# Layer 0 scores of two-block tiles as two half-width products of 64 queries and 192 keys

## The chip, the cores and the metric

The kernel runs on one core of one Trainium2 chip. The metric is the device time in microseconds of one execution. The engines are named as the profile names them: PE is TensorE (PEld its weight loads, which overlap its products), DVE is VectorE, ACT is ScalarE, POOL is GpSimd, SP is SyncE, whose queue issues most DMAs. Each engine runs its own instructions in order and waits for the others by semaphores.

## What is computed

Two transformer layers, both modulated by a conditioning vector, on `x` of 2 batches x 512 positions x 512 channels in float32. Each layer is an attention and a feed-forward part, each behind a layer norm with gain and shift, each added back through a gate. The change touches only the attention of layer 0: 32 query heads share 8 key/value heads, 128 channels a head, with a sliding window of 128 positions.

```python
q = _rope((x @ wq).reshape(B, S, 32, 128), pos)
k = _rope((x @ wk).reshape(B, S, 8, 128), pos)
v = (x @ wv).reshape(B, S, 8, 128)
qg = q.reshape(B, S, 8, 4, 128)
scores = jnp.einsum('bqhgd,bshd->bhgqs', qg, k) * sm_scale
allowed = (j <= i) & (j > i - 128)
scores = jnp.where(allowed[None, None, None], scores, neg)
attn = jax.nn.softmax(scores, axis=-1)
out = jnp.einsum('bhgqs,bshd->bqhgd', attn, v)
return out.reshape(B, S, 32 * 128) @ wo
```

A query at position i sees the keys i-127 to i. For a block of 128 queries these lie in its own block of 128 keys and the one before.

## The kernel before

**Layer 0's attention** (`attention0`, L529) works in 16 units, one for each pair of key/value head and batch. A unit has four blocks of 128 queries (`qb` 0 to 3). The loop over steps `n` (inside `tc.manual_schedule`, L678) takes one block a step and spreads the work of a block over three steps. The order in which it issues is the order of each engine's queue. In step `n` come: `scores` of block `n`; keys, values or queries of the next unit (`keys`, `values`, `queries`, through `roped`, L548); `normalised` of block `n`; `turned` of block `n-1` (transposes of the probabilities); `output` of block `n-2` (projection by `wo`, added to `x`); `mix` of block `n-1` (probabilities times values). At the end of early steps comes one piece of the modulation vectors, popped from `aside`: every third piece is a group of products for the modulation rows (`mod_rows`, L96), the piece after it transposes them (`mod_columns`, L114), and other pieces load weights or spread the gates. In the last units, pieces of layer 0's feed-forward part follow.

So on PE a score tile stands between `mix` of the block before (L650, four 512-column records) and the queries, keys or values of the next unit (L552, L574). Only where an `aside` piece ended the step before does that piece stand ahead of it.

**A score tile** (`scores`, L598). For block 0 there is one key block (`nk` = 128), for the others two (`nk` = 256). For each of the four heads of the unit there is one product: 128 queries as weights, `nk` keys as the moving operand, into the PSUM tile `sp` of 128 x 4 x 256 float32. DVE adds the mask table `band` (L610; 0 where a query may look, -1e30 elsewhere) and takes the negative maximum (L616). ACT takes the exponential with the sum of each row, head by head (L620), into an SBUF tile. `sp` comes from a pool with a single buffer (L543), so the products of a tile can start only when ACT has read the tile before.

In a two-block tile the 128 x 256 scores of a head hold two corners that the mask removes whole: the first 64 queries never see the last 64 keys, the last 64 queries never the first 64 keys.

**Products on part of the columns.** A product whose weights have at most 64 or 32 columns can be put on part of the array's columns, chosen by the PSUM partitions that it writes. The kernel does so in `mod_rows` (L103: 32 weight columns, two products side by side) and in layer 1's `mix` (L1102: 32 columns, four side by side). The profile writes such shapes as 128*32, the full one as 128*128.

**Before the loop** the modulation rows of the first norm, the norm itself and its transposes run, `tables` (L506) loads the rotation table and `band`, and `load_group` (L514) the weights of the first head.

Of the kernel before, what the change touches and what calls it, by code (L numbers as in the profile page):

```python
# [10 lines left out]
F32 = mybir.dt.float32  # L11
F32R = mybir.dt.float32r
I32 = mybir.dt.int32
AF = mybir.ActivationFunctionType
ALU = mybir.AluOpType
AX = mybir.AxisListType
PSUM = bass.MemoryType.PSUM

P = 128
# [4 lines left out]
EPS = 1e-5  # L24

NKV, GRP, HD, WIN = 8, 4, 128, 128

NH, HD1, LAT, ROPE = 128, 4, 64, 64
SCALE1 = float(1.0 / np.sqrt(np.float32(HD1 + ROPE)))
# [13 lines left out]
def adaln_kernel(ctx: ExitStack, tc: tile.TileContext, A: dict, out: bass.AP):  # L43
# [247 lines left out]
    with ExitStack() as c01:  # L291
# [7 lines left out]
        with ExitStack() as c00:  # L299
# [34 lines left out]
            def finale(ap, pool):  # L334
# [31 lines left out]

            norm1 = Norm(1, 0, 1, mid)
            attention0(
                tc, small, hT, xs, gate[2], ident, tabs, groups, load_group,
                lambda pool: [  # L370
# [124 lines left out]
def weights0(tc, A, ctx):  # L495

    nc = tc.nc
    wq = A["L0_attn_wq"].rearrange("(kc p) n -> p kc n", p=P)
    wk = A["L0_attn_wk"].rearrange("(kc p) n -> p kc n", p=P)
    wv = A["L0_attn_wv"].rearrange("(kc p) n -> p kc n", p=P)  # L500
    wo = A["L0_attn_wo"].rearrange("(h p) n -> p h n", p=P)
    QW = GRP * HD
    wp = ctx.enter_context(tc.tile_pool(name="w0", bufs=2))
    tab = ctx.enter_context(tc.tile_pool(name="tab0", bufs=1))

    def tables():  # L506

        rope = tab.tile([P, 4, S], F32, tag="rope", name="rope")
        nc.sync.dma_start(out=rope, in_=A["c_rope"])
        band = tab.tile([P, 2 * P], F32, tag="band", name="band")  # L510
        nc.sync.dma_start(out=band, in_=A["c_band"])
        return rope, band

    def load_group(g):  # L514
        w = {}
        w["k"] = wp.tile([P, KC, HD], F32, tag="wk", name=f"wk{g}")
        nc.sync.dma_start(out=w["k"], in_=wk[:, :, g * HD : (g + 1) * HD])
        w["v"] = wp.tile([P, KC, HD], F32, tag="wv", name=f"wv{g}")
        nc.sync.dma_start(out=w["v"], in_=wv[:, :, g * HD : (g + 1) * HD])
        w["q"] = wp.tile([P, KC, QW], F32, tag="wq", name=f"wq{g}")  # L520
        nc.sync.dma_start(out=w["q"], in_=wq[:, :, g * QW : (g + 1) * QW])
        w["o"] = wp.tile([P, GRP, D], F32, tag="wo", name=f"wo{g}")
        nc.sync.dma_start(out=w["o"], in_=wo[:, g * GRP : (g + 1) * GRP, :])
        return w

    return tables, load_group


def attention0(tc, small, hT, xs, ga, ident, tabs, groups, load_group, aside, finale):  # L529
# [7 lines left out]
    nc = tc.nc  # L537
    rope, band = tabs
    units = [(g, b) for g in range(NKV) for b in range(B)]
    NU = len(units)  # L540
    with ExitStack() as ctx:
        ap = ctx.enter_context(tc.tile_pool(name="a0", bufs=2, reuse_waits="tile"))
        pss = ctx.enter_context(tc.tile_pool(name="pss0", bufs=1, space=PSUM, reuse_waits="tile"))  # L543
        pst = ctx.enter_context(tc.tile_pool(name="pst0", bufs=2, space=PSUM, reuse_waits="tile"))
        pmm = ctx.enter_context(tc.tile_pool(name="psm0", bufs=4, space=PSUM, reuse_waits="tile"))
        kTs, vs, qTs, oTs, sps, pes, pTs = ({} for _ in range(7))

        def roped(dst, wcols, b, tables, name):  # L548

# [44 lines left out]
        def window(qb):  # L594
            k0 = max(qb - 1, 0)
            return k0, (qb + 1 - k0) * P

        def scores(u, qb):  # L598

            k0, nk = window(qb)  # L600
            sp = pss.tile([P, GRP, 2 * P], F32, tag="s", name=f"s{u}_{qb}")
            for hh in range(GRP):
                nc.tensor.matmul(  # L603
                    sp[:, hh, :nk],
                    lhsT=qTs[u][:, hh, qb * P : (qb + 1) * P],
                    rhs=kTs[u][:, k0 * P : k0 * P + nk],
                    start=True,
                    stop=True,
                )
            nc.vector.tensor_add(  # L610
                sp[:, :, :nk],
                sp[:, :, :nk],
                band[:, 2 * P - nk :].unsqueeze(1).to_broadcast([P, GRP, nk]),
            )
            nm = small.tile([P, GRP], F32, tag="nm", name=f"nm{u}_{qb}")
            nc.vector.tensor_reduce(nm, sp[:, :, :nk], AX.X, ALU.max, negate=True)  # L616
            pe = ap.tile([P, GRP, 2 * P], F32, tag="p", name=f"p{u}_{qb}", bufs=3)
            rs = small.tile([P, GRP], F32, tag="rs", name=f"rs{u}_{qb}")
            for hh in range(GRP):
                nc.scalar.activation(  # L620
                    pe[:, hh, :nk], sp[:, hh, :nk], AF.Exp,
                    bias=nm[:, hh : hh + 1], accum_out=rs[:, hh : hh + 1],
                )
            pes[u, qb] = pe, rs
# [53 lines left out]
        with tc.manual_schedule(engines=FOUR):  # L678
            for n in range(-TB, NU * TB + 2):
                u, qb = divmod(n, TB)  # L680
                new = u + 1
                if new < NU and qb == 0 and units[new][1] == 0 and new:
                    groups.append(load_group(units[new][0]))
                if 0 <= u < NU:
                    scores(u, qb)
                if new < NU:
                    if qb == 0:
                        keys(new)
                        queries(new, 0)
                    elif qb == 1:  # L690
                        values(new)
                        queries(new, 1)
                    else:
                        queries(new, qb)
                if 0 <= u < NU:
                    normalised(u, qb)
                before, last = divmod(n - 1, TB), divmod(n - 2, TB)
                if 0 <= n - 1 < NU * TB:
                    turned(*before)
                if 0 <= n - 2:  # L700
                    output(*last)
                if 0 <= n - 1 < NU * TB:
                    mix(*before)
                if aside and n >= -3:
                    aside.pop(0)()
                for f in steps.get(n, ()):
                    f()
# [540 lines left out]
def _constants():  # L1248

    half = HD // 2  # L1250
    inv = np.float32(10000.0) ** (-np.arange(half, dtype=np.float32) / np.float32(half))
    ang = np.arange(S, dtype=np.float32)[None, :] * inv.astype(np.float32)[:, None]
    cos, sin = np.cos(ang).astype(np.float32), np.sin(ang).astype(np.float32)
    co = np.concatenate([cos, cos])

    si = np.concatenate([sin, -sin])
    sm = np.float32(HD**-0.5)
    rope = np.stack([co * sm, si * sm, co, si], axis=1).astype(np.float32)

    i, j = np.arange(P)[:, None], np.arange(2 * P)[None, :]  # L1260
    band = np.where((j > i) & (j <= i + WIN), 0.0, -1e30).astype(np.float32)

    r = np.arange(P) % 16
    lowq = (r // 4 % 2 == 1).astype(np.float32)
    lowk = (r // 8 == 1).astype(np.float32)
    cols = np.zeros((P, 12), np.float32)
    cols[:, 8:] = np.arange(P)[:, None] // 16 % 4 == np.arange(4)[None, :]
    cols[:, 0] = r % 8 < 4
    cols[:, 1] = r % 8 >= 4
    cols[:, 2], cols[:, 3] = 2 * lowq - 1, lowq  # L1270
    cols[:, 4], cols[:, 5] = 2 * lowk - 1, lowk

    i, j = np.arange(P)[:, None], np.arange(P)[None, :]
    blocks = np.arange(P)[:, None] % 16 == np.arange(16)[None, :]
    heads = np.arange(P)[:, None] // 16 % 2 == np.arange(2)[None, :]
    spread = np.stack(
        [(i // 8 == j // 8) & (i % 8 // 2 == 2 * (1 - ty)) for ty in range(2)], axis=1
    ).astype(np.float32)
    n, m = np.arange(N1)[:, None], np.arange(N1)[None, :]
    before = np.broadcast_to((m < n).astype(np.float32), (P, N1, N1)).copy()  # L1280
    expert = np.broadcast_to((np.arange(E1 * R) // R).astype(np.float32), (N1, E1 * R)).copy()
    return {
        "c_rope": rope, "c_band": band, "c_cols": cols, "c_spread": spread,
        "c_block": blocks.astype(np.float32), "c_head": heads.astype(np.float32),
        "c_before": before, "c_expert": expert,
    }
# [46 lines left out]
```

## Time and profile before

| | us |
|---|---|
| median of 3 runs | 2598.6 (2596.83 to 2599.06) |
| the profiled execution, its own time | 2598.26 |
| span of the profiled execution, first to last instruction | 2596.5 |
| PE busy, 60 to 940 us (layer 0's attention and its feed-forward part) | 866.2 of 880 |
| DVE busy there | 460.8 |
| ACT busy there | 178.3 |
| POOL busy there | 306.1 |
| one step of a full unit with two key blocks, 491.19 to 502.38 us (score tile to score tile) | 11.19 |

How to read the profile: the busy time of an engine is the union of its instructions' times. A PE record's duration includes its way through the array, so records of a stream overlap; what a record costs the stream is the distance from its start to the next one's. In the order of time, equal neighbours are merged into one line: start, length from the first start to the last end, engine, line of the kernel, operation, output<-inputs, shape (rows*columns of the array, then the moving operand) and count. A bracket at the end of a line gives the engine's idle time before it and what ended that. In the groups the last figures are busy us, mean ns of one | idle us before. In a list of waits they are us in total, times, longest us.

### The profile page before, as it was taken

The page shows a single profiled execution, that of the slowest core. Times are in us where ns is not written, and L with a number is a line of the kernel's source. Part 1 is how long each engine was busy: PE and PEld are TensorE (multiplying, and loading weights), DVE is VectorE, ACT ScalarE, POOL GpSimd, SP SyncE. Part 2 cuts the span into 40 slices and gives each one's busy share as a digit, 9 for nine tenths or more (in the row PEclk, how much of TensorE's full clock was granted, in tenths as well). Part 3 has the DMA queues.
Part 4 walks back from the last instruction along what each step waited for, and adds up shares of the span by engine and source line. Part 5 has one row for each costly group of instructions (what it writes and reads, how often), then busy time and mean ns, then how long its engine had stood idle before and what let it go on. Part 6 is the DMA issues. An engine that isn't in the chain of part 4 may idle for free.

```text
span 2596.5 us, 32803 instructions
## 1 busy us (share of the span) xinstructions
PE 2501.8 (96%) x12316; PEld 1353.1 (52%) x12316; DVE 1712.8 (66%) x2390; ACT 1443.2 (56%) x2151; POOL 1593.2 (61%) x1538
## 2 busy tenths in 40 slices
PE   7999999999998999999999999999999999999757
PEld 3555555555555445555555555555555555555333
DVE  4455555555555247777778878787877887887642
ACT  2212211211112127888888888888888888888610
POOL 1333334333333315888888888888888888888841
PEclk9999999999999999999999999999999999999868
DMA  6211101101000110000000010000010000000010
GB/s 231 87 57 49 41 9 33 41 7 34 17 1 5 29 32 27 18 25 25 25 25 20 23 29 25 25 17 25 25 29 25 18 24 25 25 29 9 1 31 33
DMA packets 68575, 81.72 MB, mean 31 GB/s; under 512 B 6881, under 2 KB 49536, under 8 KB 68288
## 3 DMA queue, kind: packets, MB, share of 16 engines
q1 hardware_dynamic: 68064, 79.34, 9.8%
q8 instruction: 97, 1.59, 0.3%
q14 instruction: 62, 0.51, 0.1%
q0 software_dynamic: 352, 0.28, 0.0%
HBM read 77.51 MB, written 2.10 MB: 31 GB/s over the span
## 4 chain that ended last, share of the span: by engine, by line
PE 92%; DVE 2%; issue 2%; POOL 1%; ACT 1%; DMA 1%; SPq 0%; POOLq 0%; DVEq 0%; ACTq 0%
PE s L946 20%; PE psq L872 17%; PE acc L1102 9%; PE ps_q L552 8%; PE pw L664 8%; PE s L955 5%; PE s L603 4%; PE po L650 4%; PE psv L574 2%; PE ps_k L552 2%; PE psm L1025 2%; PE pt L639 2%; PE psu L895 2%; PE psf L275 1%; PE psw L1158 1%
## 5 line engine op out<-in xcount | busy, mean ns | idle before, releaser
L1052 POOL TENSOR_TENSOR ss<-ss,row 128x512 f32<-128x512 f32 x512 | 652.8, 1288 | 51.7 <-ACT row L1037 51.3
L965 ACT COPY ss<-s 128x1024 f32<-128x1024 f32 x512 | 506.7, 1013 | 105.6 <-PE s L955 79.9
L1055 ACT ACTIVATE ss<-ss 128x1024 f32<-128x1024 f32 x512 | 530.7, 1066 | 8.0 <-POOL ss L1052 8.0
L872 PE MATMUL psq<-hT,wqr 128*128 128x512 f32 x1024 | 466.9, 599 | 0.1
L620 ACT ACTIVATE p<-s,nm 128x256 f32<-128x256 f32 (+1 forms) x256 | 110.9, 445 | 488.6 <-DVE nm L616 479.8
L972 DVE TENSOR_TENSOR mx<-s,mx 128x1024 f32<-128x1024 f32 x256 | 307.0, 1220 | 97.7 <-PE s L955 96.7
L1046 POOL TENSOR_TENSOR ss<-ss,rowe 128x512 f32<-128x512 f32 x256 | 327.8, 1291 | 2.3 <-ACT rowe L1041 2.3
L562 POOL TENSOR_TENSOR qT<-t_q,t_q 128x512 f32<-128x512 f32 x64 | 81.2, 1269 | 402.6 <-DVE t_q L561 402.6
L872 PEld LDWEIGHTS psq<-hT,wqr 128*128 128x128 f32 x1024 | 189.1, 190 | 242.7 <-issue 216.8
L1102 PE MATMUL acc<-ss,vp 128*32 128x512 f32 x2048 | 266.6, 607 | 7.9 <-ACT ss L1055 7.8
L946 PE MATMUL s<-qh,chkr 64*128 64x512 f32 x1024 | 243.7, 437 | 10.6 <-ACT ss L965 7.4
L972 DVE TENSOR_TENSOR mx<-s,ss 128x1024 f32<-128x1024 f32 x128 | 156.8, 1225 | 113.3 <-PE s L955 90.5
L664 PE MATMUL pw<-wo,oT 128*128 128x512 f32 x512 | 230.3, 592 | 0.0
L552 PE MATMUL ps_q<-hT,wq 128*128 128x512 f32 x512 | 230.1, 592 | 0.0
L955 PE MATMUL s<-qm,c 64*128 64x512 f32 x1024 | 218.4, 391 | 0.0
L946 PE MATMUL s<-ql,clkr 64*128 64x512 f32 x1024 | 218.2, 391 | 0.0
L946 PE MATMUL s<-qh,clkr 64*128 64x512 f32 x1024 | 218.0, 392 | 0.0
L946 PE MATMUL s<-ql,chkr 64*128 64x512 f32 x1024 | 217.8, 392 | 0.0
L946 PEld LDWEIGHTS s<-qh,chkr 64*128 64x128 f32 x1024 | 105.8, 184 | 154.2 <-issue 77.5
L1015 POOL TENSOR_TENSOR st<-mh,own_block 128x512 fp32r<-128x512 f32 x64 | 67.2, 1050 | 180.5 <-DVE mh L1011 180.5
L977 DVE STREAM_TRANSPOSE mx<-mx 128x1024 f32<-128x1024 f32 x128 | 158.7, 1240 | 2.2
L1048 DVE TENSOR_TENSOR ss<-ss,psm 128x512 f32<-128x512 f32 x256 | 158.2, 680 | 0.7 <-PE psm L1025 0.7
(207 smaller groups left out, 3934.8 us busy)
## 6 DMA issues: line engine op xcount, KB each, us to landing
wqr<-in_L_attn_Wq_rope_pairs SPq DMA_DIRECT2D x64, 512.0 KB
wmod<-in_L_wmod SPq DMA_DIRECT2D x12, 1024.0 KB
wq<-in_L_attn_wq SPq DMA_DIRECT2D x8, 1024.0 KB
wo<-in_L_attn_wo SPq DMA_DIRECT2D x8, 1024.0 KB
x<-in_L_attn_x SPq DMA_DIRECT2D x8, 256.0 KB
wk<-in_L_attn_wk SPq DMA_DIRECT2D x8, 256.0 KB
wv<-in_L_attn_wv SPq DMA_DIRECT2D x8, 256.0 KB
wT<-in_L_ffn_WT SPq DMA_DIRECT2D x2, 1024.0 KB
```

Of the source, the lines that this page charges most:

```text
L552: nc.tensor.matmul(ps, lhsT=wcols(kc), rhs=hT[b][:, kc, :], start=(kc == 0), stop=(kc == KC - 1))
L664: nc.tensor.matmul(ps, lhsT=oTs[u][:, hh, i * P : (i + 1) * P], rhs=groups[g]["o"][:, hh, :], start=(hh == 0), stop=(hh == GRP - 1),)
L872: nc.tensor.matmul(ps, lhsT=wqs[t][:, kc, pair * P : (pair + 1) * P], rhs=hT[b][:, kc, :], start=(kc == 0), stop=(kc == KC - 1),)
L946: nc.tensor.matmul(out[:, j, :], lhsT=k[b]["kr"][r, bass.ts(i, P)], rhs=q[t, p][r, :], start=(n == 0), stop=False,)
L955: nc.tensor.matmul(out[:, j, :], lhsT=qkc[t // 2, 1][r, bass.ts(i, P)], rhs=qm[t, p][r, :], start=False, stop=True,)
L965: nc.scalar.copy(ss[t, i, p], hold["s", t, i, p])
L972: nc.vector.tensor_max(mx[t, p], hold["s", t, i, p], before)
L977: nc.vector.transpose(m, m)
L1046: nc.gpsimd.tensor_sub(s, s, hold["r", t, 2])
L1052: nc.gpsimd.tensor_sub(s, s, hold["r", t, 2 * p + 1])
L1055: nc.scalar.activation(ss[t, i, p], ss[t, i, p], AF.Exp)
L1102: nc.tensor.matmul(accs[g, b][32 * h : 32 * (h + 1), :], lhsT=vps[t][:, kb, h, :], rhs=ss[t, kb, h // 2][:, h % 2, :], start=(s == 0 and k ...
```

## The change

In a tile with two key blocks, each head's product of 128 queries with 256 keys becomes two: queries 0 to 63 with keys 0 to 191, and queries 64 to 127 with keys 64 to 255. Each has 64 weight columns and writes 64 PSUM partitions. Tiles with one key block keep their single product of 128 queries and 128 keys, but write it into the right half of `sp`.

The corners that are no longer computed must not reach the maximum and the exponential. So `sp` is made once, ahead of the loop, and filled with -1e30 by DVE; the mask table has 0 in these corners, so that adding it leaves -1e30 there. A one-block tile writes its scores into columns 128 to 255, where one of the two corners lies; its own mask, which is now a third block of `band`, sets that corner back to -1e30. All 128 partitions and all `nk` columns are added, reduced and exponentiated as before. The offsets move: the valid columns start at `o` = 256 - `nk`.

```diff
+H2 = P // 2
+NEVER = -1e30
...
-        band = tab.tile([P, 2 * P], F32, tag="band", name="band")
+        band = tab.tile([P, 3 * P], F32, tag="band", name="band")
...
+        sp = pss.tile([P, GRP, 2 * P], F32, tag="s", name="scores")
+        nc.vector.memset(sp, NEVER)
...
             k0, nk = window(qb)
-            sp = pss.tile([P, GRP, 2 * P], F32, tag="s", name=f"s{u}_{qb}")
-            for hh in range(GRP):
-                nc.tensor.matmul(
-                    sp[:, hh, :nk],
-                    lhsT=qTs[u][:, hh, qb * P : (qb + 1) * P],
-                    rhs=kTs[u][:, k0 * P : k0 * P + nk],
+            o = 2 * P - nk
+            for hh in range(GRP) if qb == 0 else ():
+                nc.tensor.matmul(
+                    sp[:, hh, o:],
+                    lhsT=qTs[u][:, hh, :P],
+                    rhs=kTs[u][:, :P],
                     start=True,
                     stop=True,
                 )
+            for hh in range(GRP) if qb else ():
+                for h in range(2):
+                    lo, hi = h * H2, 2 * P - (1 - h) * H2
+                    nc.tensor.matmul(
+                        sp[h * H2 : (h + 1) * H2, hh, lo:hi],
+                        lhsT=qTs[u][:, hh, qb * P + h * H2 : qb * P + (h + 1) * H2],
+                        rhs=kTs[u][:, k0 * P + lo : k0 * P + hi],
+                        start=True,
+                        stop=True,
+                    )
             nc.vector.tensor_add(
-                sp[:, :, :nk],
-                sp[:, :, :nk],
-                band[:, 2 * P - nk :].unsqueeze(1).to_broadcast([P, GRP, nk]),
+                sp[:, :, o:],
+                sp[:, :, o:],
+                band[:, 0 if qb else 2 * P :][:, :nk].unsqueeze(1).to_broadcast([P, GRP, nk]),
             )
...
-            nc.vector.tensor_reduce(nm, sp[:, :, :nk], AX.X, ALU.max, negate=True)
+            nc.vector.tensor_reduce(nm, sp[:, :, o:], AX.X, ALU.max, negate=True)
...
-                    pe[:, hh, :nk], sp[:, hh, :nk], AF.Exp,
+                    pe[:, hh, :nk], sp[:, hh, o:], AF.Exp,
...
-    band = np.where((j > i) & (j <= i + WIN), 0.0, -1e30).astype(np.float32)
+    band = np.where((j > i) & (j <= i + WIN), 0.0, NEVER).astype(np.float32)
+    band = np.concatenate([band, band[:, P:]], axis=1)
+
+    band[:H2, 2 * P - H2 : 2 * P] = 0.0
+    band[H2:, :H2] = 0.0
```

More of the change, by code (lines that the diff above doesn't have):

```diff
@@ L545, in attention0 @@
         pmm = ctx.enter_context(tc.tile_pool(name="psm0", bufs=4, space=PSUM, reuse_waits="tile"))
-        kTs, vs, qTs, oTs, sps, pes, pTs = ({} for _ in range(7))
+        kTs, vs, qTs, oTs, pes, pTs = ({} for _ in range(6))
+        sp = pss.tile([P, GRP, 2 * P], F32, tag="s", name="scores")
+        nc.vector.memset(sp, NEVER)
         def roped(dst, wcols, b, tables, name):
```

## The prediction

> **What bounds the kernel now.** I read the page's busy shares first, then its chain of waits, then the groups of the stretch in which layer 0's attention runs, its waits, and last the order of time around single tiles. From the page (rows 1 and 4):
>
> ```profile
> PE 2501.8 (96%) x12316; PEld 1353.1 (52%) x12316; DVE 1712.8 (66%) x2390; ACT 1443.2 (56%) x2151; POOL 1593.2 (61%) x1538
> ...
> PE 92%; DVE 2%; issue 2%; POOL 1%; ACT 1%; DMA 1%; SPq 0%; POOLq 0%; DVEq 0%; ACTq 0%
> ```
>
> TensorE is busy for 96% of the span and makes 92% of the chain that ended last; the score products of layer 0 (L603) alone are 4% of that chain. Between 60 and 940 us, groups by form (busy us, mean ns | idle before):
>
> ```profile
> L603 PE MATMUL s<-kT,qT 128*128 128x256 f32 x384 | 91.3, 381 | 0.0
> ...
> L603 PE MATMUL s<-kT,qT 128*128 128x128 f32 x120 | 15.9, 276 | 0.0
> ...
> L103 PE MATMUL psr<-wmod,sc 128*32 128x512 f32 x64 | 14.5, 595 | 0.0
> ```
>
> No idle before any of them. TensorE's own waits in this stretch:
>
> ```profile
> PE po L650 <- ACT pT L641: 8.2, 4, 5.5
> PE pst L193 <- DVE xn L184: 2.8, 1, 2.8
> PE pst L193 <- ACT hT L203: 2.4, 1, 2.4
> ```
>
> That is 13.4 us in 880, the longest (5.5 us at 832 us) in the last unit. So in this stage a microsecond taken from TensorE is a microsecond of the time, except beside those few waits. The clock granted there is 0.99, so the durations need no correction.
>
> One undisturbed step of a two-block tile (the order of time on TensorE; start us, us, line):
>
> ```profile
> 500.66 1.88 PE L650 MATMUL po<-pT,v 128*128 128x512 f32 x4
> 502.38 1.89 PE L603 MATMUL s<-kT,qT 128*128 128x256 f32 x8
> 504.10 3.60 PE L552 MATMUL ps_q<-hT,wq 128*128 128x512 f32 x8
> ```
>
> Durations overlap, so starts count. A float32 product shows as two records. Start to start: four 512-column records in 1.72 us, 0.429 each; eight 256-column records in 1.72 us, 0.216 each. Where 128 columns follow each other (the transposes L639) it is 0.109. So a record costs 2.5 ns + 0.833 ns per column, and one of 192 columns would take 0.1625 us.
>
> The trace has no product on a half of the columns (128*64), but two groups on quarters (128*32): the modulation rows L103, which use two quarters at once, and layer 1's mix L1102, which uses four. One L103 group stands directly between `po` and a score tile:
>
> ```profile
> 199.18 1.88 PE L650 MATMUL po<-pT,v 128*128 128x512 f32 x4
> 200.99 3.63 PE L103 MATMUL psr<-wmod,sc 128*32 128x512 f32 x16
> 204.54 1.99 PE L603 MATMUL s<-kT,qT 128*128 128x256 f32 x8
> 206.37 1.02 PE L552 MATMUL ps_q<-hT,wq 128*128 128x512 f32 x2
> ```
>
> Sixteen 512-column records take 3.55 us, not 16 x 0.429 = 6.86: they run as eight pairs, whose members start 7 ns apart, each pair 0.429 after the last. But both borders cost something. From the single records, to the nanosecond: the last `po` to the first L103 is 0.523 instead of 0.429 (**0.094** more), the first pair to the second 0.453 (0.024 more: the first weights, 32 columns, are not loaded ahead); last pair to first score record 0.528 (0.100 more, of which 7 ns is the stagger), first to second score record 0.320 instead of 0.216 (**0.104** more: 128 columns of weights in the open). The same 0.094 stands at the other changes of array shape that I looked at in layer 1 (0.522 instead of 0.429 from L1102 to L872 and from L872 to L946). The open load is 0.024 for 32 columns and 0.104 for 128, so about 0.051 for 64.
>
> **The change, part by part.**
>
> *The products.* 16 units x 3 tiles = 48 tiles change. Before: 4 heads x 2 records x 0.216 = 1.727 us. After: 4 heads x 2 halves x 2 records of 192 columns; if the halves run as pairs, 8 x 0.1625 = 1.300. That gives back 0.427 us a tile, 20.5 us in all.
>
> *The borders.* Each changed tile now stands alone in another shape: in, 0.094 + 0.051; out, 0.100 + 0.104; together 0.349. Nothing hides this: TensorE is the bound, and the stall is in its own array. 42 tiles therefore gain 0.427 - 0.349 = 0.078 us each, 3.3 us. The other six (steps 2, 3, 5, 6, 9, 11) stand behind an L103 group or behind the 64-row transposes L119 that follow it, and pay for a border already; these take 1.831 us from their first record to the next line now and would take 1.300 + 0.051 + 0.100 + 0.104 = 1.555, a gain of 0.276 each, 1.7 us. Sum 4.9 us; about 0.2 of it falls beside the late 5.5 us wait. I take **4.7 us**.
>
> Here a rule of the Trainium skill speaks against the change. TensorEngine Tiling (Array Packing), Key Properties, says that changing the tiling mode drains the engine, and gives no price. Without it the sum would be -20.5 us; with the row's price it is -4.9. I take the row: the shape differs only in 64 for 32. A second rule, in Instruction Overhead on the same page, puts about 60 cycles on every matmul. At 2.4 GHz (Trainium Kernel Development and Optimization, NeuronCore Architecture), 25 ns, the eight extra records of a tile would cost 0.2 us, 9.6 us over 48 tiles, and turn the sum to +4.9. The trace does not bear it out: the fixed part of a record is 2.5 ns, and a second member of an L103 pair moves the next pair by nothing.
>
> *Weight loads.* 16 loads of 64 columns instead of 8 of 128. By the slope above one takes 0.053 us, so even one after the other a pair's two take 0.107, inside the 0.1625 of the pair before; L103 shows that loads run a pair ahead in this mode. Cost 0; if they were not hidden, up to 0.107 x 7 = 0.7 us a tile.
>
> *The score tile made once.* It was already a single buffer. The waits stay as they were, now perhaps by head: the first product of a tile needs the exponentials of the tile before, which end at 508.7 us for a product at 513.6. Cost 0, cover some 5 us.
>
> *The memset.* One DVE write of 128x1024 to PSUM; the nearest row (L616, the same tile) takes 1.22 us. It can start when the earlier users of these banks are done, near 28.5 us, and would push the first `t_k`; DVE sits idle for 1.34 us before `t_q` at 31.96, and the keys are not used before 57. Cost 0, without that cover 1.2.
>
> *The larger table.* `c_band` grows from 128 to 192 KB: 65.5 KB at the 231 GB/s of the first slice is 0.28 us in front of the weights of group 0. It is still one DMA of SP's queue. The first key product waits for ACT and DVE (`hT`), not for a DMA; cost 0, otherwise 0.3. Add, maximum and exponential keep their sizes; only offsets change.
>
> **Sum.** The profiled execution took 2598.26 us for a span of 2596.5, and lies 0.3 below the median of 2598.6. 2598.26 - 4.7 = 2593.6; against the median 2593.9. **I predict 2593.8 us.** The measurement tells about 0.2% (5.2 us) from no change, so this forecast sits almost on the border, at 2593.4.
>
> **Rivals.**
> - *The borders cost less or nothing* (6%): if the array does not drain between the full shape and halves, up to 20.5 us are gained: 2578. For it: no 128*64 row exists to refute it. Against: every change of shape that I looked at shows the 0.094. With half of them, 48 x 0.175 = 8.4 us more: 2585.
> - *TensorE's instruction supply becomes the bound* (slower, 20%). A changed tile is 32 instructions (16 loads, 16 products) to be started in 1.30 us, 41 ns each. The densest 32 of the trace of before stand in 1.45 us, the densest 64 in 3.29 (45 and 51 ns). If the latter is a rate and not just what that code asks for, a tile's body is 32 x 51 = 1.64 us, 0.34 more: 48 x 0.34 = 16 us more, 2610; at 45 ns 7 us more, 2601. It decides from 0.43 - 0.35 = 0.08 us a tile, a body of 1.38, or 43 ns. Against: at the start of an L1102 group twelve instructions start within 50 ns, so a stock is held, and the `po` before a score tile (8 instructions in 1.7 us) gives time to fill it.
> - *The halves do not run together* (6%): 16 x 0.1625 = 2.60 us a tile, 48 x 1.30 = 62 us more: 2656. For it: no row with 64-column halves. Against: L103 and L1102. A milder form, in which only a product's second record overlaps the next half's first, makes nine rows of eight: +0.16 a tile, 2601.6, still within the border (3%). L103's first pair, started together, speaks against it.
>
> **How the numbers follow.** Forecast 65%, from 2590 to 2597 by the error of the borders (0.05 us a tile is 2.4 us); about half of it lies below 2593.4. Faster by over 0.2%: 0.40 (34 from the forecast, 6 from cheaper borders). Within 0.2%: 0.38 (31 from the forecast, 3 from the milder overlap, 4 from a supply limit near 45 ns). Slower by over 0.2%: 0.22 (16 from the supply limit, 6 from halves one after the other). The range that leaves out no more than 2 in 10 takes the forecast, the mild overlap and most of the supply case: 2588 to 2609; the forecast's own is 2590 to 2597.
>
> **What would show it.** In the profile after: L603 with 128*64 and 192 columns, 768 records; pairs 7 ns apart and 0.1625 us from pair to pair (products right); 0.52 from the last `po` and about 0.21 from the first pair to the second (way in); 0.26 from the last pair to the next line, whose second record is 0.104 late (way out). First record to next line: 1.55 us for 1.73. A pair period of 0.2 or more means supply or loads; single starts mean no overlap. I am wrong if the borders of this shape differ from those of quarters, or if TensorE's waits in the stage grow past 14 us.

## The result and the profile after

| | before | after |
|---|---|---|
| median of 14 runs each, us | 2598.35 | 2592.68 |
| lowest and highest | 2596.83, 2599.49 | 2590.83, 2595.83 |
| span of the profiled execution | 2596.5 | 2591.0 |

The ratio is 0.998, 95% interval 0.9972 to 0.9987: between 3.4 and 7.3 us faster, with the medians 5.7 apart. The forecast was 4.7 us under the profiled execution, and 2593.8 as a time.

The groups by form between 60 and 940 us, after the change (the columns as before; L620 is the product of the halves, L610 that of the one-block tiles, L558 that of the queries, which was L552):

```profile
L620 PE MATMUL scores<-kT,qT 128*64 128x192 f32 x768 | 73.0, 332 | 0.0
L610 PE MATMUL scores<-kT,qT 128*128 128x128 f32 x120 | 15.9, 276 | 0.0
L105 PE MATMUL psr<-wmod,sc 128*32 128x512 f32 x64 | 14.5, 595 | 0.0
L558 PE MATMUL ps_q<-hT,wq 128*128 128x512 f32 x480 | 218.9, 599 | 0.0
```

The queries before:

```profile
L552 PE MATMUL ps_q<-hT,wq 128*128 128x512 f32 x480 | 215.8, 592 | 0.0
```

The 384 records of 256 columns were busy for 91.3 us; the 768 records of 192 columns take 73.0 between them. The difference of 18.3 us is three times what the kernel gained, so the group alone is misleading: part of the cost shows in the lines beside it, as in the 3.1 us more of the queries. One step shows where. The order of time of the profile after, on TensorE, around the same tile as before:

```profile
496.73 1.88 PE L667 MATMUL po<-pT,v 128*128 128x512 f32 x4
498.54 1.52 PE L620 MATMUL scores<-kT,qT 128*64 128x192 f32 x16
499.99 3.70 PE L558 MATMUL ps_q<-hT,wq 128*128 128x512 f32 x8
503.53 1.04 PE L656 MATMUL pt<-ident,p 128*128 128x128 f32 x8
```

Read the starts. From `po` to the scores 1.81 us instead of 1.72: the way in. From the first score to `ps_q` 1.45 instead of 1.72. From `ps_q` to the transposes 3.54 instead of 3.44: the open load on the way out, which now falls into the line behind the tile. Together the stretch is 6.80 us instead of 6.88. TensorE's waits in this stage, after:

```profile
PE po L667 <- ACT pT L658: 8.1, 4, 5.6
PE pst L195 <- DVE xn L186: 2.8, 1, 2.8
PE pst L195 <- ACT hT L205: 1.4, 1, 1.4
```

12.3 us instead of 13.4; nothing new waits.

### The profile page after: what moved, and what is told of

The parts are those of the page before. It is cut to its first block, busy times and chain, and to the rows that moved or that the text cites. A ratio compares the mean times of both kernels' runs of the same rounds, so it can differ in the third digit from the quotient of the medians.

```text
span 2591.0 us, 33543 instructions
## 1 busy us (share of the span) xinstructions
PE 2501.0 (97%) x12700; PEld 1328.9 (51%) x12700; DVE 1712.8 (66%) x2391; ACT 1444.3 (56%) x2151; POOL 1595.1 (62%) x1538
## 4 chain that ended last, share of the span: by engine, by line
PE 92%; DVE 2%; issue 2%; POOL 1%; ACT 1%; DMA 1%; POOLq 0%; DVEq 0%; ACTq 0%
PE s L963 20%; PE psq L889 17%; PE acc L1119 9%; PE ps_q L558 9%; PE pw L681 8%; PE s L972 5%; PE po L667 4%; PE scores L620 3%; PE psv L580 2%; PE ps_k L558 2%; PE psm L1042 2%; PE pt L656 2%; PE psu L912 2%; PE psf L277 1%; PE psw L1175 1%
## 5 line engine op out<-in xcount | busy, mean ns | idle before, releaser
L637 ACT ACTIVATE p<-scores,nm 128x256 f32<-128x256 f32 (+1 forms) x256 | 111.2, 446 | 480.2 <-DVE nm L633 471.2
L558 PE MATMUL ps_q<-hT,wq 128*128 128x512 f32 x512 | 233.3, 598 | 0.0
```

Source lines behind the costliest of these rows:

```text
L558: nc.tensor.matmul(ps, lhsT=wcols(kc), rhs=hT[b][:, kc, :], start=(kc == 0), stop=(kc == KC - 1))
```

## The experiments

Eight runs, all compared with the kernel before on the same chip. Lines and edits refer to the kernel after the change. Per-tile figures are start to start, from the single records of the trace; a float32 product is two records there. The name behind a heading is that by which later texts refer to the run.

**The change without its halves.** (`e1_whole`)

```diff
-            for hh in range(GRP) if qb == 0 else ():
+            for hh in range(GRP):
                 nc.tensor.matmul(
                     sp[:, hh, o:],
-                    lhsT=qTs[u][:, hh, :P],
-                    rhs=kTs[u][:, :P],
+                    lhsT=qTs[u][:, hh, qb * P : (qb + 1) * P],
+                    rhs=kTs[u][:, k0 * P : k0 * P + nk],
...
-            for hh in range(GRP) if qb else ():
-                for h in range(2):
...
-    band[:H2, 2 * P - H2 : 2 * P] = 0.0
-    band[H2:, :H2] = 0.0
```

> The change without its halves: the score tile made once and filled, the wider table and the new offsets stay, but every two-block tile is again one product of 128 queries and 256 keys per head. Theory (the gain is the halves' 0.078 us a tile and nothing else): as before the change, 2598.4 within 1. Rival (the about 1 us by which the measured gain exceeds the sum, 5.7 against 4.7, comes from the other edits, at the start or by finer waits): 2597.4, and the first changed tile again some 0.6 us earlier than before the change.

Measured: 2597.17 us against 2597.55, ratio 1.0 (0.9991 to 1.0008). The single tile, its memset, the wider table and the offsets are worth nothing that these runs can tell; the gain belongs to the halves. The interval of about 2 us on either side can't decide between the theory and the rival's 1 us. The trace helps with the start: here too TensorE reaches the first score tile 0.39 us earlier than in the profile of before, and the first transposes of the modulation (L121) 0.33; in the changed kernel it was 0.27 and 0.70. Up to the first two-block tile the nine traces taken of changed kernels have the same work on TensorE, and they reach it between 65.85 us (the change itself) and 67.23 us (the quarters, second run), for 66.46 before. So such tenths at the start come and go from one execution to the next, and need no edit to explain them.

**The borders alone.** (`e2_wide`)

```diff
-                    lo, hi = h * H2, 2 * P - (1 - h) * H2
+                    lo, hi = 0, 2 * P
...
-    band[:H2, 2 * P - H2 : 2 * P] = 0.0
-    band[H2:, :H2] = 0.0
```

> Halves of 64 queries, but each over all 256 keys: the borders are paid and nothing is saved in the products. Theory (borders 0.349 us a tile for 42 tiles, 0.151 for the six behind an L105 group or its transposes): +15.6 us, 2614. Pairs 0.216 us apart. Rival (borders and open loads depend on the length of the products at their sides): another price than 0.349 in the records, and a time off 2614 by more than 2.

Measured: 2611.94 us against 2597.55, ratio 1.0056 (1.0042 to 1.0069), so 14.4 us slower. Its order of time, `po`, scores and what follows:

```profile
497.71 1.02 PE L667 MATMUL po<-pT,v 128*128 128x512 f32 x2
498.66 1.95 PE L620 MATMUL scores<-kT,qT 128*64 128x256 f32 x16
500.54 2.84 PE L558 MATMUL ps_q<-hT,wq 128*128 128x512 f32 x6
```

Eight pairs, 0.216 us apart, would take 1.727; from the first score to `ps_q` it is 1.878, of which 0.051 is the first open load and 0.100 the border on the way out. With 0.094 ahead of the tile and 0.104 behind, the price of a tile's borders is 0.348 us. It is what rows of 32 columns and of 512 had promised for one of 64 columns beside one of 256: the price doesn't depend on the length of these products. The sum, 15.6 us, is 1.2 above the medians' difference, which is inside the interval (10.9 to 17.9). The 2614 on record is off by 2.1, just past the 2 that the text allowed; it started from 2598.4, and from this group's 2597.55 the sum is 2613.2.

**Quarters.** (`e3_quarters`)

```diff
-H2 = P // 2
+H2 = P // 4
...
-                for h in range(2):
-                    lo, hi = h * H2, 2 * P - (1 - h) * H2
+                for h in range(4):
+                    lo, hi = h * H2, h * H2 + WIN + H2
...
-    band[:H2, 2 * P - H2 : 2 * P] = 0.0
-    band[H2:, :H2] = 0.0
+    for h in range(4):
+        band[h * H2 : (h + 1) * H2, : h * H2] = 0.0
+        band[h * H2 : (h + 1) * H2, h * H2 + WIN + H2 : 2 * P] = 0.0
```

> Four products of 32 queries and 160 keys per head instead of two of 64 and 192. Theory (the stream sets the pace, and four quarters run side by side as in L1119): eight rows of 0.136 us, borders 0.094 + 0.024 + 0.114 + 0.104, 1.42 us a tile instead of 1.727; 15.8 us under before the change, 2582.6. Rival (instruction supply: a tile is 64 instructions in 1.09 us, 17 ns each, while the changed kernel has shown 41 ns each): 64 x 41 ns = 2.6 us for the rows, 1.2 us a tile more than before the change, some 2655; or anything between, with rows wider than 0.136 us after the first stock is used up.

Measured: 2581.69 us against 2597.55, ratio 0.9941 (0.9929 to 0.9954): 15.9 us faster, on the forecast. This settles the supply rival, by a load twice as dense as the change's:

```profile
432.70 1.02 PE L667 MATMUL po<-pT,v 128*128 128x512 f32 x2
433.65 1.29 PE L620 MATMUL scores<-kT,qT 128*32 128x160 f32 x32
434.88 2.41 PE L558 MATMUL ps_q<-hT,wq 128*128 128x512 f32 x5
```

32 product records, and as many weight loads, in 1.22 us. The rows start 0.136 us apart to the last one; nothing widens. The densest 64 instructions of the kernel before (3.29 us) were no rate of the machine, only what that code asked for. That decides it for tiles of this size. Whether a stock of instructions, filled while `po` runs, carries the whole tile is not shown, since no run asks for this density over longer than one tile.

The second run of the same kernel (`e3_again`):

> The quarters once more, beside the two kernels of this group: 2581.7, 15.8 under before the change. Theory and rival as for the first run of it; it serves as the base of e5_turned.

2582.24 us against 2598.26, the same ratio of 0.9941 (0.9928 to 0.9955).

**Another order of the halves.** (`e4_order`)

```diff
-            for hh in range(GRP) if qb else ():
-                for h in range(2):
+            for h in range(2) if qb else ():
+                for hh in range(GRP):
                     lo, hi = h * H2, 2 * P - (1 - h) * H2
```

> The same sixteen half products of a tile in another order: the first halves of all four heads, then the second halves. Theory (products start in the order in which they are issued, and two overlap only where neighbours in that order lie on different column halves): nearly no pairs, sixteen records of 0.1625 us less one overlap, 2.4 to 2.6 us a tile; +1.0 to +1.3 us a tile against before the change, 2648 to 2661. Rival (each half has a queue of its own and takes what is its): pairs as in the change, 2592.7.

Measured: 2625.83 us against 2597.55, ratio 1.0107 (1.0093 to 1.0121). 28 us slower than before, where the theory had 50 or more and the rival a gain: both were wrong.

```profile
504.27 1.02 PE L667 MATMUL po<-pT,v 128*128 128x512 f32 x2
505.22 2.22 PE L620 MATMUL scores<-kT,qT 128*64 128x192 f32 x16
507.37 2.84 PE L558 MATMUL ps_q<-hT,wq 128*128 128x512 f32 x6
```

2.15 us from the first score to `ps_q` for 1.45 in the change; 48 x 0.70 is 33.6 us, and 2592.7 + 33.6 = 2626.3. The starts of this tile's sixteen records fall into two chains with steps of 0.1625 us, each with its own open load at the head:

```
505.223 505.437 505.599 505.762 505.924 506.087 506.249 506.412
505.930 506.143 506.306 506.468 506.631 506.793 506.956 507.118
```

The first chain has to be the first halves, the second the second halves, since a half runs one record at a time. All eight first halves come ahead in the order of issue, yet the second chain starts at 505.930, when the fifth record of the first has just started and three of it have not. So three records can be held back for a busy half while those behind them go to the other; as long as four were held, the other half stood idle. This is also how the change's order gives pairs at all: both records of a head's first half come ahead of those of its second, the second record is held, and the other half starts 7 ns after the first.

**Two heads at a time.** (`e6_twos`)

```diff
-            for hh in range(GRP) if qb else ():
-                for h in range(2):
+            for h2 in range(4) if qb else ():
+                h = h2 % 2
+                for hh in range(2 * (h2 // 2), 2 * (h2 // 2) + 2):
                     lo, hi = h * H2, 2 * P - (1 - h) * H2
```

> The halves in the order first half of heads 0 and 1, second half of heads 0 and 1, then the same for heads 2 and 3, so that four records of one half stand in a row. Theory (from e4_order: the other half starts only when three records of the half in front are still to start, so some three records can be held back): the second half starts together with the first or one record later; 2593 to 2600. Rival (only the next product is held back, and what stands behind it waits): the second half starts two or more records late in each group of four, and a tile takes twelve rows or so: 0.6 us a tile more than the change, some 2622.

Measured: 2594.62 us against 2598.26, ratio 0.9987 (0.998 to 0.9994). Four records of a half stand in a row: one runs, three are held, and the second half starts 13 ns after the first. The tile takes 1.50 us for 1.45. The 0.05 is where the second half turns to heads 2 and 3: there its record is 0.370 us long instead of 0.326 and its next start 0.207 away instead of 0.1625, as behind a load that came late; that cause is not shown. The count of three agrees with both orders; how the hold is built was not tried.

**Transposes right behind the scores,** on the quarters. (`e5_turned`)

```diff
                 if 0 <= u < NU:
                     scores(u, qb)
+                before, last = divmod(n - 1, TB), divmod(n - 2, TB)
+                if 0 <= n - 1 < NU * TB:
+                    turned(*before)
...
-                before, last = divmod(n - 1, TB), divmod(n - 2, TB)
-                if 0 <= n - 1 < NU * TB:
-                    turned(*before)
```

> The quarters, with the transposes of the block before moved up to stand right behind the scores. Theory (the open load on the way out is the first weights of what follows: 0.104 us for 128 columns of a product, 0.055 for a transpose, as in the last unit of the changed kernel, where transposes follow): 0.05 us in each of the 45 tiles that had a product behind them, 2.2 us under the quarters. Rival (the probabilities of the block before, ready by POOL only shortly before, are now waited for, or the copies of the transposes by ACT and DVE come behind the new tile's exponentials and hold up mix): TensorE waits of several us in all, no gain or a loss.

Measured: 2586.18 us, ratio 0.9951 (0.9939 to 0.9964): still faster than before, but slower than the quarters (2582.24 in the same group). Set beside the trace of the quarters' second run, each later step that begins with a two-block tile does gain 0.04 to 0.05 us, as the theory had it; but by step 2 it is 4 us behind. The list of waits from 50 to 100 us has the rival's wait, once:

```profile
PE pt L656 <- POOL p L647: 3.4, 1, 3.4
PE psg L144 <- DVE grow L135: 2.1, 1, 2.1
```

And behind it (stretches with busy time of the engines, then the granted clock, DMA share and GB/s):

```profile
66.00:70.70 4.70, 1.33 (x34) 0.95 (x33) 4.41 (x6) 0.00 (x0) 2.47 (x3) 0.89 0.00 0
70.70:77.50 6.80, 6.80 (x36) 6.80 (x37) 0.18 (x1) 2.41 (x9) 0.00 (x0) 0.57 0.01 2
77.50:84.00 6.50, 6.50 (x22) 2.34 (x22) 2.72 (x5) 0.59 (x1) 0.61 (x1) 1.00 0.14 40
```

Behind the wait the granted clock is 0.57 for 6.8 us. The 32 product records of the values (L580) took 5.9 us there, for 3.7 in the quarters' trace. The rule in the Trainium skill, TensorE: Matmul & The Clock Gate, Part 1, that the clock halves after an idle window of some 3.4 us, fits this wait: behind one of 1.09 us at 819 us in the profile after, the clock is 1.00. The length of a wait alone does not decide, though. Of the two waits of 2.8 us for `xn` in the lists above, the one in the profile before ended at 921.39 us and had 4.9 us at 1.00 behind it; the one in the profile after ended at 916.05 us and had 10.1 us at 0.50.

**The same, but not in step 1.** (`e7_turned_late`)

```diff
+                before, last = divmod(n - 1, TB), divmod(n - 2, TB)
+                if 1 < n <= NU * TB:
+                    turned(*before)
...
-                before, last = divmod(n - 1, TB), divmod(n - 2, TB)
-                if 0 <= n - 1 < NU * TB:
+                if n == 1:
                     turned(*before)
```

> As e5_turned, but the transposes stay in their old place in step 1, where they waited 3.4 us for POOL and TensorE's clock fell to 0.57 for the 7 us behind it. Theory (this one wait and the slow clock after it ate a steady gain of 0.049 us a step): no wait on the probabilities, no slow stretch near 71 us, and 2.2 us under the quarters, 2580. Rival (the move costs in the steady steps too, or the wait only moves to step 2): 2582 or more, with a wait of the transposes on POOL in the list.

Measured: 2579.65 us against 2598.43, ratio 0.9929 (0.9916 to 0.9943), 18.8 us faster, the fastest of all. The list of waits has no transposes on POOL; its first lines, and a line from the order of time in the last unit, are:

```profile
PE po L667 <- ACT pT L658: 9.3, 5, 5.8
PE pst L195 <- DVE xn L186: 3.0, 2, 2.8
...
799.86 1.98 PE L667 MATMUL po<-pT,v 128*128 128x512 f32 x4 [0.59 <-ACT pT L658]
```

The rival's other wait is there, though: `mix` waits five times for the copies of the transposes, 9.3 us in all, where the quarters have four such waits and 8.7 us. Against the quarters' second trace the move gains 2.05 us from the first two-block tile to step 60, and loses 0.80 by step 61, where the new wait of 0.59 stands. The move of the transposes is worth 2.6 us by the two medians, 2.2 by the theory's sum; the two intervals overlap, so of this pair of runs alone one could not say that it gained.

## Why the prediction was right, point by point

**The bound.** Right: the 0.078 us that a tile saves on TensorE are 0.078 in the distance from step to step (498.543 - 487.435 = 11.108 us after, 11.186 before), from one end of the units to the other.

**The products.** Right, to the nanosecond where it can be seen: pairs 7 ns apart, 0.1625 us from pair to pair, 768 records of 192 columns in the shape 128*64, which the trace of before did not contain. At this period the loads are hidden, and the 60 cycles a record that the prediction weighed do not show. (The estimate made from them should have been +4.7 us, 9.6 less 4.9, and not +4.9.)

**The borders.** Right: 0.094 in, 0.051 of open load, 0.100 out, 0.104 of open load; 0.523 from the last `po`, 0.213 from the first pair to the second and 0.263 from the last pair to the next line, in the records of the tile at 498.54. The borders-alone run measured the price by itself. They eat 0.349 of the 0.427 us that the smaller products bring, which is why a change that takes a quarter of the score products' columns away moves the time by 0.2%.

**The six tiles behind a modulation group.** Right. The tile at 80.3 us stands in the order of time as

```profile
80.30 1.52 PE L620 MATMUL scores<-kT,qT 128*64 128x192 f32 x16
81.75 3.70 PE L558 MATMUL ps_q<-hT,wq 128*128 128x512 f32 x8
```

and gains 0.276: 1.831 us became 1.451, less the 0.104 in the line behind. Its entry still costs 0.094 us (0.522 for 0.429): quarters to halves is a change of shape too.

**The late wait.** Wrongly sized. The sum let 0.2 us fall beside it; the trace shows 0.8. TensorE was 5.80 us ahead of the old trace at 823 us, and 5.04 ahead at the last tile:

```profile
832.23 3.78 PE L667 MATMUL po<-pT,v 128*128 128x512 f32 x4 [5.61 <-ACT pT L658]
835.81 1.82 PE L195 MATMUL pst<-ident,xn 128*128 128x128 f32 x8
837.56 1.52 PE L620 MATMUL scores<-kT,qT 128*64 128x192 f32 x16
```

The wait itself is only 0.13 us longer than before (5.48). The rest is clock: `po` ran at 0.50 behind the wait in both traces, but the transposes L195 behind it ran at 0.54 and took 1.75 us to the next line, where they had 0.78 and 1.12 in the trace of before. The working priced a wait by its length, and left out the clock behind it. The other traces show that this part is not the halves' doing. With two heads at a time, after a wait of 5.56 us, these transposes took 1.20 us to the next line; without halves 1.14; in both traces of the quarters 0.97; with the transposes right behind the scores 1.73. It varies with where the slow stretch of the clock lies, from one execution to the next.

**The edits costed at nothing.** The memset came where it was put: at 28.72 us, 0.91 long (the estimate was 1.22), between the first operations on `t_k`. DVE's idle time before `t_q` shrank to 0.21 us, so nothing behind it moved. The waits on the score tile and the larger table show up nowhere; the first run above bounds these edits together to about 2 us either way.

**The sum.** 4.7 was forecast and 5.7 measured, by medians whose interval is 3.4 to 7.3. In the two traces the balance is: 0.6 us ahead when the first two-block tile starts, within the spread of the other traces there and so no work of the halves (the granted clock from 59 to 60 us is 0.92 in this trace, 0.50 in that of before); 5.2 more by 823 us, for 4.9 in the sum (0.1 of the rest is that in the last unit transposes follow a tile, with an open load of 0.056 instead of 0.104; another 0.14 is a wait for ACT that shrank); 0.8 lost at the late wait; then back from 5.04 to 5.5 by the end, over the last tile and layer 1, which the change doesn't touch. What lies outside the score tiles is less than these runs can resolve. The two parts that the sum did not have, 0.6 at the start and 0.8 at the late wait, nearly cancel in this pair of traces: that the total came within a microsecond is in part luck, the 0.078 us a tile is not.

**The rivals.** Cheaper borders: refuted by the borders-alone run and by every tile. Instruction supply: refuted by the quarters. Halves one after the other: refuted for this order; the other order shows that the rival had a real mechanism and only the wrong place. The milder overlap (the other half starting with a product's second record) would be true if nothing could be held back; three records can.

## What to carry to other kernels

Before a product is split over parts of the array, price the two borders from any other change of shape in the same trace (here 0.094 us each, plus the first weights in the open at about 0.8 ns per column), and set them against what one visit saves: the visit must be long, or save much, or stand beside work of the same shape. Issue the parts in turn, product by product; the same products part by part cost some 33 us more. And a densest stretch seen in a trace can be a demand and not a limit: where the rival is a supply limit, a run with a denser demand decides it, and here it was also the better kernel.

## What the runs showed of the hardware that was not expected

- **Products start out of order across parts of the array.** Three records were held for a busy half while later ones started on the other. So what is said at the head, that each engine runs its instructions in order, has an exception here. The Trainium skill, TensorE: Matmul & The Clock Gate, Part 3, states that matmuls are strictly first in, first out in start and end. The starts in the other-order run contradict it for parts of the array's columns; the measurement decides. For the end nothing contradicts it: in the tile below, the record that signals the tile's end starts at 81.700 us and four of its records start behind it, the last at 81.935 (0.299 long), yet DVE, which waits for that signal, starts at 82.31.
- **It even mixes two lines of code.** In the quarters, a score tile behind a modulation group has the same shape, and its two free quarters start before the group's last pair:

```profile
77.52 3.20 PE L105 MATMUL psr<-wmod,sc 128*32 128x512 f32 x14
80.13 0.47 PE L620 MATMUL scores<-kT,qT 128*32 128x160 f32 x4
80.55 0.60 PE L105 MATMUL psr<-wmod,sc 128*32 128x512 f32 x2
80.98 1.26 PE L620 MATMUL scores<-kT,qT 128*32 128x160 f32 x28
```

  The first score record starts 6 ns behind the pair ahead: where the shape doesn't change, no border is paid. Three records are held on each of the two busy quarters here (one of the group's last pair, two of the first head), so the count of three is one for each part, not for the whole array.
- **A transpose's weights are cheap in the open:** 0.056 us for 128 columns, against 0.104 for the weights of a product.
- **A wait of 3.4 us cost TensorE 2.2 us more behind it,** in 32 small product records at a granted clock of 0.57, so waits of about this length should be priced with a possible aftermath.
